# State sums for two quads at once, a last image kept on chip, and a new plan: a state-space layer and its feed-forward part on one core

## The chip, the core and the metric

One core of one Trainium2 chip. Times are device microseconds (us). TensorE is PE (PEld: its weight loads), VectorE DVE, ScalarE ACT, GpSimd POOL, SyncE SP; SP issues the DMA transfers. Every run named here was in the fast state. A ratio of two kernels is the mean time of one kernel's fast runs over that of the other's in the same rounds, so it is not quite the ratio of the medians that I quote.

## The reference, cut to what matters

```python
# x: (8, 384, 32, 32), all float32; per image 1024 tokens of 384 channels
t = layernorm(...)                                  # per token
xm, z = split(t @ in_proj_w.T)                      # 768 + 768
xc = silu(causal_conv3(xm))
dt, Bm, Cm = split(xc @ x_proj_w.T)                 # 24, 16, 16
dt = softplus(dt @ dt_proj_w.T + b)
h = exp(dt * A) * h + (dt * xc) * Bm                # scan over 1024 tokens, 768 x 16 states
y = (sum over the 16 states of h * Cm + xc * D) * silu(z)
x = x + gelu(y @ out_proj_w.T @ mlp_w1.T + b1) @ mlp_w2.T + b2
# images 0..4 only: binarised feed-forward with absmax quantisation, W1 (1536 x 384), W2 (384 x 1536)
```

## The kernel before

The kernel describes its work as operations with an engine, a cost and a priority. A greedy planner in the kernel simulates the engines, places every operation, and emits the instructions in that order. On the chip each engine then follows its own fixed order; semaphores make it wait for data and buffers. The planner's constants and its numbers of buffers therefore decide the order of everything.

```python
MM = 0.86; SWITCH = 0.34; BATCH = 1; IDLE = 0.7; SLACK = 1.0
# Plan.run, PE: a planned idle stretch above IDLE is filled with filler matmuls ("spare")
while now - free[e] > IDLE and ...: self.fill(); free[e] = clock.run(free[e], MM / 2)
# rings of buffers
"w_f": 4, "w_b": 4, "res": 3, "u": 6, "dt_r": 3, "dtx_r": 3, "front": 2, "yg": 1
"da": 2 (PSUM), "y": 1 (PSUM), "mm": 3 (PSUM)
```

The scan takes the 16 states in four quads. One tile has 32 channels x 4 states on its partitions:

```python
def scan_tile(...):
    ACT : da = exp(dt_r * a_neg)
    POOL: u = dtx_r * B
    DVE : to = tensor_tensor_scan(da, u)             # to is da, or u on a POOL tile
    DVE or POOL: u = to * C
# per quad: sum the 4 states of 32 channels; 4 column tiles of 32, fp32
def sums():
    for q, hcs in batch:                              # BATCH quads
        for p0, hc in parts:                          # 4 matmuls
            nc.tensor.matmul(py[p0:p0 + 32, :], self.fold, hc, start=(q == 0), stop=(q == 3))
add("PE", SWITCH + BATCH * MM, sums, ...)             # op.slack = SLACK
# then: xr = xr * D + py (DVE); xr = xr * z (POOL); store to yg_d in HBM
# s3: load yg from HBM; p_out: 3 x 6 matmuls; p_h: 36; p_o: 36 (per half image)
# s1: norms of both halves first; gates (p_z) late; x_proj and dt_proj weights resident in SBUF
[...]
```

Lines of lower priority fill PE between the sums: the projections of later images (p_in, p_z), out_proj and MLP of earlier ones (p_out, p_h, p_o), the feed-forward part (p_y). What is left of them when the last sums are done runs at the end.

## Time and profile before

| | before |
|---|---|
| median (3 runs) | 3439.42 us (3437.82 to 3448.25) |
| profiled span | 3444.9 us |
| busy PE / DVE / POOL / ACT | 96 / 84 / 77 / 59% |
| PE idle; fillers; half clock | 142 us; 128 us; PE busy 151 us at half rate |
| first sums, last sums | 130 us, 3345 us |

A group line names source line, engine, operation, tiles and shape, then the count, busy us, mean ns, and after the second bar the idle time of that engine before these instructions and who ended it. The prediction shows the lines. One more is needed later, from a table of windows; its columns are length, busy us of PE, PEld, DVE, ACT and POOL with counts, granted clock, DMA share, GB/s. It covers images 1 and 2 (from the first sums of image 1 to those of image 3) of the kernel before:

```profile
614.00:1424.00 810.00, 791.01 (x2610) 324.79 (x2606) 720.28 (x514) 477.22 (x488) 647.64 (x311) 0.99 0.68 224
```

PE is busy for 791 of 810 us here. It looks like the bound.

### The profile page before, as it was taken

Reading aid. Unit: us, or ns where it says so; the run is one execution under the profiler, and the core shown is the slowest. Engines: PE = TensorE matmul, PEld = TensorE weight load, DVE = VectorE, ACT = ScalarE, POOL = GpSimd, SP = SyncE. Lnnn points to the kernel's source line nnn. Section 1 sums busy time; section 2 is a strip of 40 time slices with the busy share of each in tenths; the row PEclk is TensorE's granted clock in tenths of the full one; section 3 lists DMA queues with packets and bytes.
Section 4 is the critical chain, followed back from the end, with each engine's and each line's share of the span. In section 5 each row is a group of like instructions: output and inputs, shape, how many; then the busy total and the mean of one; then the engine's idle time right before and its main releaser. Section 6 shows DMA issues by size and latency. Waiting matters only on the chain.

```text
span 3444.9 us, 32879 instructions
## 1 busy us (share of the span) xinstructions
PE 3302.8 (96%) x10500; PEld 1326.3 (38%) x10500; DVE 2885.8 (84%) x2193; ACT 2019.7 (59%) x2295; POOL 2655.3 (77%) x1288
## 2 busy tenths in 40 slices
PE   8888898999999999999999999999899999999999
PEld 3333433434343334333333333333333433333344
DVE  3577789899899989789989989899998899789870
ACT  4676567556666565554565656655576554555541
POOL 1778777777897968689777888788898779878850
PEclk9889899999999999999999999999999999999999
DMA  5876757667686557765588665986577666766542
GB/s 192 259 237 210 242 179 231 200 207 248 228 285 200 198 191 259 240 215 188 206 270 278 221 204 184 304 248 215 177 269 250 199 201 208 238 190 206 182 138 69
DMA packets 363965, 746.30 MB, mean 217 GB/s; under 512 B 34832, under 2 KB 103952, under 8 KB 363792
## 3 DMA queue, kind: packets, MB, share of 16 engines
q1 hardware_dynamic: 361776, 743.31, 66.6%
q8 instruction: 84, 1.38, 0.2%
q10 hardware_dynamic: 2016, 0.88, 0.1%
q14 instruction: 89, 0.73, 0.1%
HBM read 560.56 MB, written 183.50 MB: 216 GB/s over the span
## 4 chain that ended last, share of the span: by engine, by line
PE 61%; DVE 12%; DMA 8%; ACT 8%; POOL 5%; issue 5%; SPq 1%; DVEq 0%; POOLq 0%; ACTq 0%
PE p_y L454 14%; PE p_o L454 11%; PE p_h L454 10%; PE py L745 7%; DVE da L812 7%; PE p_out L454 6%; PE p_in L454 4%; PE p_z L454 4%; ACT da L470 3%; POOL u L808 2%; DVE u L825 2%; PE p_dbc L630 2%; ACT L470 1%; PE p_sum L483 1%; DMA dt_r<-dt_d 1%
## 5 line engine op out<-in xcount | busy, mean ns | idle before, releaser
L808 POOL TENSOR_TENSOR u<-dtx_r,bc 128x1024 f32<-128x1024 f32 x768 | 1796.8, 2359 | 493.7 <-PE py L745 418.9
L812 DVE TENSOR_TENSOR_SCAN da<-da,u 128x1024 f32<-128x1024 f32 (+1 forms) x576 | 1163.9, 2021 | 187.3 <-ACT da L470 113.0
L470 ACT ACTIVATE da<-dt_r,a_neg 128x1024 f32<-128x1024 f32 (+1 forms) x960 | 903.1, 946 | 687.8 <-DVE u L825 571.8
L825 DVE TENSOR_TENSOR u<-da,bc 128x1024 f32<-128x1024 f32 x576 | 703.2, 1221 | 25.2 <-DVE da L812 0.9
L454 PE MATMUL p_h<-t,w_b 128*128 128x512 f32 x1152 | 519.9, 601 | 12.2 <-ACT g L470 9.4
L454 PE MATMUL p_o<-g,w 128*128 128x512 f32 x1152 | 513.8, 598 | 1.2 <-DMA w<-in_mlp_w 1.0
L822 POOL TENSOR_TENSOR u<-u,bc 128x1024 f32<-128x1024 f32 x192 | 452.7, 2358 | 66.6 <-DVE u L812 46.1
L745 PE MATMUL py<-u,fold 128*32 128x512 f32 x3072 | 427.9, 611 | 15.7 <-POOL u L822 15.4
L812 DVE TENSOR_TENSOR_SCAN u<-da,u 128x1024 f32<-128x1024 f32 (+1 forms) x192 | 384.3, 2011 | 45.8 <-ACT da L470 29.8
L454 PE MATMUL p_y<-gf,w_n 128*128 128x512 f32 x720 | 328.9, 610 | 12.7 <-DMA w_n<-bin_w 8.2
L454 PEld LDWEIGHTS p_h<-t,w_b 128*128 128x128 f32 x1152 | 212.2, 190 | 315.0 <-issue 252.0
L454 PE MATMUL p_y<-tn,w_b 128*128 128x512 f32 x720 | 328.4, 605 | 1.0 <-ACT dt L470 0.8
L454 PEld LDWEIGHTS p_o<-g,w 128*128 128x128 f32 x1152 | 213.6, 190 | 299.9 <-issue 288.2
L470 ACT ACT_TABLE_LOAD x223 | 286.1, 1283 | 8.4 <-DVE xc L601 4.7
L454 PE MATMUL p_out<-yg,w 128*128 128x512 f32 x576 | 267.3, 616 | 16.8 <-DMA yg<-yg_d 9.6
L454 PE MATMUL p_in<-t,w_f 128*128 128x512 f32 x504 | 232.3, 608 | 10.3 <-ACT halo L596 6.0
L454 PE MATMUL p_z<-t,w_f 128*128 128x512 f32 x504 | 231.1, 607 | 2.3 <-ACT dt L470 1.3
L454 PEld LDWEIGHTS p_y<-gf,w_n 128*128 128x128 f32 x720 | 136.2, 194 | 204.0 <-issue 186.4
L454 PEld LDWEIGHTS p_y<-tn,w_b 128*128 128x128 f32 x720 | 134.1, 192 | 192.4 <-issue 154.0
L812 DVE TENSOR_TENSOR_SCAN da<-da,state,u 128x512 f32<-128x512 f32 x144 | 185.0, 1284 | 19.0 <-ACT da L470 7.0
L470 ACT ACTIVATE y<-p_y,v_b 128x512 f32<-128x512 f32 x150 | 101.8, 684 | 150.8 <-PE p_y L454 103.6
L601 DVE SCALAR_TENSOR_TENSOR xc<-p_in,conv_w,xc 128x511 f32<-128x511 f32 (+1 forms) x192 | 140.7, 742 | 54.2 <-ACT xc L470 32.6
(94 smaller groups left out, 2777.9 us busy)
## 6 DMA issues: line engine op xcount, KB each, us to landing
dtx_r<-dtx_d SPq DMA_DIRECT2D x144, 512.0 KB, 5.1
dt_r<-dt_d SPq DMA_DIRECT2D x144, 512.0 KB, 5.2
w_b<-in_mlp_w SPq DMA_DIRECT2D x192, 192.0 KB, 2.8
w<-in_mlp_w SPq DMA_DIRECT2D x96, 384.0 KB, 3.4
w_f<-in_in_proj_w SPq DMA_DIRECT2D x168, 192.0 KB, 4.5
y_d<-y SPq DMA_DIRECT2D x120, 256.0 KB, 3.8
gf<-y_d SPq DMA_DIRECT2D x20, 1536.0 KB, 9.2
xc_d<-xc SPq DMA_DIRECT2D x32, 768.0 KB, 7.5
```

What stands on the lines that cost most here:

```text
L454: self.nc.tensor.matmul(p.real, w.real[:, k, :], t.real[:, k0 + k, :], start=start and k == 0, stop=stop and k == n - 1,)
L470: lambda: self.nc.scalar.activation(out(), in_(), func, **{k: v() if callable(v) else v for k, v in kw.items()}),
L483: nc.tensor.matmul(p_sum.real, self.ones, t.real[:, k, :], start=(k == 0), stop=(k == KC - 1))
L601: nc.vector.scalar_tensor_tensor(xc.real[:, m, s:], pm.real[:, : T - s], tap[2 - s], xc.real[:, m, s:], ALU.mult, ALU.add,)
L630: nc.tensor.matmul(p_dbc.real, self.x_w[:, k, :], xc.real[:, k, :], start=(k == 0), stop=(k == KD - 1),)
L745: nc.tensor.matmul(py.real[p0 : p0 + DQ, :], self.fold, hc, start=(q == 0), stop=(q == NQUAD - 1),)
L808: add("POOL", 2.36, lambda: nc.gpsimd.tensor_mul(u.real, dtx_r.real, spread(bq)), r=[dtx_r, bq], w=[u])
L812: add("DVE", 0.13 + n * 0.0021, lambda k=k, col=col: nc.vector.tensor_tensor_scan(to.real[:, k, :], da.real[:, k, :], u.real[:, k, :], sta ...
L822: add("POOL", 2.36, lambda: nc.gpsimd.tensor_mul(u.real, u.real, spread(cq)), r=[cq], w=[u])
L825: add("DVE", 1.21, lambda: nc.vector.tensor_mul(u.real, da.real, spread(cq)), r=[da, cq], w=[u])
```

## The change

The intent: pay TensorE's change of tiling mode once for two quads; give the scan nine u tiles to make that possible, and find the memory for them by streaming the x_proj and dt_proj weights, by smaller rings and by dropping a constant tile (spread); spare the last image its trip of yg through HBM; warm TensorE's clock in the opening; move small work off DVE and POOL. The norm of a half and its gates move next to that half. All this is planned anew.

```diff
-BATCH = 1
+BATCH = 2
-SLACK = 1.0
+SLACK = 1.6
@@ Plan.run
+        free["PE"] = 2 * SIGNAL                       # fillers may stand in the opening
@@ rings
-"w_f": 4, "w_b": 4, "res": 3, "u": 6
+"w_f": 3, "w_b": 3, "res": 2, "u": 9
@@ s1
-        ts = [normed(half) for half in range(2)]      # gates: gate(0) in the second half, gate(1) last
+            t = normed(half)                          # per half, and gate(half, t) at its end
-            x_proj: resident self.x_w; dt_proj: resident self.dt_w
+            x_proj, dt_proj: two loads of 192 KB each through the r_w ring, per half
@@ last image
+                add("POOL", ..., tensor_mul(yg.real[:, m, :], xr.real, zr.real))   # yg stays on chip
+                self.matmuls(pm, w, yg, 0, KD - 1, True, False, ...)              # 5 of 6 k blocks early
+                self.matmuls(pm, w, yg, KD - 1, 1, False, True, ..., KD - 1)      # the last one late
@@ small
+ state copies of POOL tiles on POOL; centring as fused multiply-add on POOL; diagonal scaled on ACT
- self.spread (constants): broadcasts of ident and ones stand in for it, in the fillers too
[...]
```

More of the change, by code (lines that the diff above doesn't have):

```diff
@@ L335, in __init__ @@
         self.rings = {
-            "front": ring("front", 2), "t_f": ring("t_f", 2), "w_f": ring("w_f", 4),
+            "front": ring("front", 2), "t_f": ring("t_f", 2), "w_f": ring("w_f", 3),
             "dbc": ring("dbc", 1), "halo": ring("halo", 2),
-            "dt_r": ring("dt_r", 3), "dtx_r": ring("dtx_r", 3), "u": ring("u", 6),
+            "dt_r": ring("dt_r", 3), "dtx_r": ring("dtx_r", 3), "u": ring("u", 9),
             "xr": ring("xr", 1), "zr": ring("zr", 1), "state": ring("state", 1),
@@ L343, in __init__ @@
             "da": ring("da", 2, psum), "y": ring("y", 1, psum),
-            "yg": ring("yg", 1), "hid": ring("hid", 2), "t_b": ring("t_b", 1), "w_b": ring("w_b", 4),
-            "w6": ring("w6", 2), "w6_n": ring("w6_n", 2), "res": ring("res", 3),
+            "yg": ring("yg", 1), "hid": ring("hid", 2), "t_b": ring("t_b", 1), "w_b": ring("w_b", 3),
+            "w6": ring("w6", 2), "w6_n": ring("w6_n", 2), "res": ring("res", 2),
             "t_n": ring("t_n", 2), "small": ring("small", 12),
@@ L374, in __init__ @@
         self.plan.fill = lambda: self.nc.tensor.matmul(
-            self.plan.spare.real[:, : 2 * P], self.ones, self.spread[:, :2, :], start=True,
-            stop=True,
+            self.plan.spare.real[:, : 2 * P], self.ones,
+            self.ones.unsqueeze(1).to_broadcast([P, 2, P]), start=True, stop=True,
         )
@@ L394, in constants @@
         )
-        self.spread = const.tile([P, G, P], F32, name="spread")
-        for g in range(G):
-            nc.vector.tensor_copy(
-                self.spread[:, g, :], ident[:, g * DQ : g * DQ + 1].to_broadcast([P, P])
-            )
         self.edge = const.tile([P, KD, 2], F32, name="edge")
@@ L422, in constants @@
         nc.vector.tensor_scalar_mul(self.a_neg, self.a_neg, -1.0)
-        self.x_w = const.tile([P, KD, P], F32, name="x_w")
-        nc.scalar.dma_start(self.x_w, a["x_proj_w"])
-        self.dt_w = const.tile([P, DI], F32, name="dt_w")
-        nc.scalar.dma_start(self.dt_w, a["dt_proj_w"])
     def load(self, to, view, src, r=(), size=0, cost=0.4):
@@ L447, in weights, with matmuls @@
         return w
-    def matmuls(self, p, w, t, k0, n, start, stop, r, claim):
+    def matmuls(self, p, w, t, k0, n, start, stop, r, claim, w0=0):
         def emit():
@@ L454, in emit @@
                 self.nc.tensor.matmul(
-                    p.real, w.real[:, k, :], t.real[:, k0 + k, :],
+                    p.real, w.real[:, w0 + k, :], t.real[:, k0 + k, :],
                     start=start and k == 0, stop=stop and k == n - 1,
@@ L519, in spread @@
             for g in range(G):
+                one = self.ident[:, g * DQ : g * DQ + 1].to_broadcast([P, P])
                 nc.tensor.matmul(
-                    p_r.real[:, g * TG : (g + 1) * TG], self.spread[:, g, :], rstd.real,
-                    start=True, stop=True,
+                    p_r.real[:, g * TG : (g + 1) * TG], one, rstd.real, start=True, stop=True
                 )
@@ L565, in normed, with gate @@
             return t
-        def gate(half):
-            t = ts[half]
+        def gate(half, t):
             z = self.piece(r_z, [P, KD, T], "z")
@@ L579, in gate @@
             by_pair("z", half, z[0])
-        ts = [normed(half) for half in range(2)]
         for half, cols in enumerate(HALVES):
-            t = ts[half]
+            t = normed(half)
             xc = self.piece(r_x, [P, KD, T], "xc")
@@ L620, in s1 @@
             by_pair("xc", half, xc[0])
-            if half:
-                gate(0)
             p_dbc = self.piece("mm", [P, T], "p_dbc")
-            def x_proj(xc=xc, p_dbc=p_dbc):
-                for k in range(KD):
-                    nc.tensor.matmul(
-                        p_dbc.real, self.x_w[:, k, :], xc.real[:, k, :],
-                        start=(k == 0), stop=(k == KD - 1),
-                    )
             dbc = self.piece("dbc", [P, T], "dbc")
-            add("PE", KD * MM, x_proj, r=all_m, w=[p_dbc], claim=[dbc])
+            for i in range(2):
+                w = self.weights(r_w, KC, a["x_proj_w"][i])
+                self.matmuls(p_dbc, w, xc, i * KC, KC, i == 0, i == 1, all_m, [dbc])
             add("ACT", 0.59, lambda dbc=dbc, p_dbc=p_dbc: nc.scalar.copy(dbc.real, p_dbc.real),
@@ L643, in s1 @@
             for k in range(KD):
+                if k % KC == 0:
+                    w = self.weights(r_w, KC, a["dt_proj_w"][k // KC])
                 i = k % DTC * DQ
                 pd = self.piece("mm", [P, T], "p_dt")
-                add("PE", MM / 2, lambda i=i, k=k, pd=pd, dbc=dbc: nc.tensor.matmul(
-                    pd.real, self.dt_w[i : i + R, k * P : (k + 1) * P], dbc.real[i : i + R, :],
+                add("PE", MM / 2, lambda i=i, k=k, pd=pd, dbc=dbc, w=w: nc.tensor.matmul(
+                    pd.real, w.real[i : i + R, k % KC, :], dbc.real[i : i + R, :],
                     start=True, stop=True,
-                ), r=[dbc], w=[pd], claim=[dt])
+                ), r=[dbc, w], w=[pd], claim=[dt])
                 self.act(
@@ L662, in s1 @@
             self.store_all("dtx", b, half, xc, all_m)
-            if half:
-                gate(1)
+            gate(half, t)
     def store_all(self, name, b, half, t, parts):
@@ L678, in s2 @@
             state = self.piece("state", [P, NJ * NQUAD], "state")
+            if b == B - 1:
+                self.last_yg = [self.piece("front", [P, KD, T], "yg") for _ in range(2)]
             for half in range(2):
@@ L778, in scan @@
             ), r=[py], w=[xr])
+            if b == B - 1:
+                yg = self.last_yg[half]
+                add("POOL", c_pool(T), lambda m=m, xr=xr, zr=zr, yg=yg: nc.gpsimd.tensor_mul(
+                    yg.real[:, m, :], xr.real, zr.real
+                ), r=[xr, zr], w=[yg[m]])
+                continue
             add("POOL", c_pool(T), lambda xr=xr, zr=zr: nc.gpsimd.tensor_mul(
@@ L817, in scan_tile @@
             c0, step = cols[0], cols[1] - cols[0]
-            add("ACT", 0.25, lambda: nc.scalar.copy(
-                state.real[:, c0 : c0 + step + 1 : step], to.real[:, :, n - 1]
-            ), r=[to], w=[state[c0]])
+            kept, last = lambda: state.real[:, c0 : c0 + step + 1 : step], n - 1
+            if on_pool:
+                add("POOL", 0.12, lambda: nc.gpsimd.tensor_copy(kept(), to.real[:, :, last]),
+                    r=[to], w=[state[c0]])
+            else:
+                add("ACT", 0.25, lambda: nc.scalar.copy(kept(), to.real[:, :, last]),
+                    r=[to], w=[state[c0]])
         if on_pool:
@@ L833, in s3 @@
         for half, cols in enumerate(HALVES):
-            yg = self.piece("yg", [P, KD, T], "yg")
-            for i in range(2):
-                src = yg_d.real[i::2, half * DP : (half + 1) * DP, :]
-                self.plan.add("SP", 0.6, lambda i=i, yg=yg, src=src: nc.sync.dma_start(
-                    yg.real[i * DP : (i + 1) * DP, :, :], src.rearrange("k p l -> p k l")
-                ), r=[yg_d[half, m] for m in range(i, NP, 2)], w=[yg[i]], size=4 * DP * KD * T)
-            t2 = self.piece("t_b", [P, KC, T], "t2")
-            for m in range(KC):
-                w = self.weights("w6", KD, a["out_proj_w"][m])
-                pm = self.piece("mm", [P, T], "p_out")
-                self.matmuls(pm, w, yg, 0, KD, True, True, [yg[0], yg[1]], [t2])
+            t2 = self.piece("t_b", [P, KC, T], "t2")
+            if b == B - 1:
+                yg = self.last_yg[half]
+                late = []
+                for m in range(KC):
+                    w = self.weights("w6_n" if m == KC - 1 else "w6", KD, a["out_proj_w"][m],
+                                     r=[yg[KC]])
+                    pm = self.piece("mm", [P, T], "p_out")
+                    self.matmuls(pm, w, yg, 0, KD - 1, True, False,
+                                 [yg[k] for k in range(KD - 1)], [t2])
+                    late.append((w, pm))
+            else:
+                yg = self.piece("yg", [P, KD, T], "yg")
+                for i in range(2):
+                    src = yg_d.real[i::2, half * DP : (half + 1) * DP, :]
+                    self.plan.add("SP", 0.6, lambda i=i, yg=yg, src=src: nc.sync.dma_start(
+                        yg.real[i * DP : (i + 1) * DP, :, :], src.rearrange("k p l -> p k l")
+                    ), r=[yg_d[half, m] for m in range(i, NP, 2)], w=[yg[i]],
+                        size=4 * DP * KD * T)
+            for m in range(KC):
+                if b == B - 1:
+                    w, pm = late[m]
+                    self.matmuls(pm, w, yg, KD - 1, 1, False, True, [yg[KD - 1]], [t2], KD - 1)
+                else:
+                    w = self.weights("w6", KD, a["out_proj_w"][m])
+                    pm = self.piece("mm", [P, T], "p_out")
+                    self.matmuls(pm, w, yg, 0, KD, True, True, [yg[0], yg[1]], [t2])
                 add("ACT", 0.59, lambda m=m, t2=t2, pm=pm: nc.scalar.copy(
@@ L936, in means @@
             )
-            nc.vector.tensor_scalar_mul(mean.real, mean.real, 1.0 / (gs * kt * P))
+            nc.vector.tensor_scalar_mul(mean.real, mean.real, -1.0 / (gs * kt * P))
         add("DVE", c_dve(used) + 0.16, means, r=[sums], w=[mean])
@@ L948, in centre @@
                         wg = w.real[:, :, lo:hi]
-                        nc.gpsimd.tensor_scalar_sub(wg, wg, mean.real[:, g : g + 1])
-            add("POOL", 2.5, centre, r=[mean], w=[w])
+                        nc.gpsimd.tensor_scalar(
+                            wg, wg, 1.0, mean.real[:, g : g + 1], ALU.mult, ALU.add
+                        )
+            add("POOL", 1.8, centre, r=[mean], w=[w])
             sgn = self.piece("hid", [P, ks.stop - ks.start, ms.stop - ms.start], "sgn")
@@ L981, in quant_scale @@
         diag, p_max = self.piece("sq", [P, P], "diag"), self.piece("mm", [P, P], "p_max")
-        def spread_out():
-            nc.vector.tensor_reduce(m1.real, mx.real, AX.X, ALU.max)
-            nc.vector.tensor_scalar_mul(diag.real, self.ident, m1.real)
-        add("DVE", 0.4, spread_out, r=[mx[k] for k in range(n)], w=[m1, diag])
+        add("DVE", 0.17, lambda: nc.vector.tensor_reduce(m1.real, mx.real, AX.X, ALU.max),
+            r=[mx[k] for k in range(n)], w=[m1])
+        self.act(lambda: diag.real, lambda: self.ident, AF.Identity, c_act(P), r=[m1], w=[diag],
+                 scale=lambda: m1.real)
         add("PE", 0.25, lambda: nc.tensor.matmul(
@@ L1149, in _laid_out @@
     rows[DTC * DQ :] = xw[R:]
-    a["x_proj_w"] = rows.reshape(P, KD, P).transpose(2, 1, 0)
+    a["x_proj_w"] = rows.reshape(P, 2, KC, P).transpose(1, 3, 2, 0)
+    a["dt_proj_w"] = a["dt_proj_w"].reshape(P, 2, KC, P).swapaxes(0, 1)
     a["D_pair"] = np.tile(np.asarray(i[c + "D"]).reshape(NP, DP).T, (2, 1))
```

## The prediction

> **What bounds the kernel now.** I read the page's first two parts, then the groups of TensorE by form, the timeline of PE in a steady stretch and at the end, a table of windows by image, and last the waits. From the page of the kernel before:
>
> ```profile
> PE 3302.8 (96%) x10500; PEld 1326.3 (38%) x10500; DVE 2885.8 (84%) x2193; ACT 2019.7 (59%) x2295; POOL 2655.3 (77%) x1288
> ...
> PE   8888898999999999999999999999899999999999
> ...
> PEclk9889899999999999999999999999999999999999
> ```
>
> PE is busy for 96% of the span, and its low slices lie among the first seven, where the granted clock is low too. DVE, at 84%, is the nearest rival. The question is what fills PE's 3303 us. The groups of PE by form (busy us, mean ns, idle before them):
>
> ```profile
> L454 PE MATMUL p_o<-g,w 128*128 128x512 f32 x1152 | 513.8, 598 | 1.2 <-DMA w<-in_mlp_w 1.0 <-ACT g L470 0.2
> L745 PE MATMUL py<-u,fold 128*32 128x512 f32 x3072 | 427.9, 611 | 15.7 <-POOL u L822 15.4 <-DVE u L825 0.2
> ...
> L374 PE MATMUL spare<-spread,ones 128*128 128x256 f32 x522 | 128.4, 393 | 0.8 <-DVE t L526 0.7
> ```
>
> Each fp32 matmul is two records (1152 are 576 matmuls). The state sums (py) come as 384 groups of 8 records, four column tiles of 32 side by side. The fillers (spare) are 261 matmuls put where the planner saw an idle PE. Before the sums PE waits 15.7 us in all, so their data is nearly always there. The timeline of PE in a steady stretch (start us, length, instructions):
>
> ```profile
> 2002.05 1.06 PE L745 MATMUL py<-u,fold 128*32 128x512 f32 x8
> 2003.05 5.42 PE L454 MATMUL p_o<-g,w 128*128 128x512 f32 x12
> 2008.40 1.06 PE L745 MATMUL py<-u,fold 128*32 128x512 f32 x8
> 2009.39 5.42 PE L454 MATMUL p_o<-g,w 128*128 128x512 f32 x12
> ...
> 2015.74 10.57 PE L454 MATMUL p_o<-g,w 128*128 128x512 f32 x24
> 2026.23 1.07 PE L745 MATMUL py<-u,fold 128*32 128x512 f32 x8
> ```
>
> Twelve more records (24 against 12) cost 10.49 - 5.35 = 5.14 us: 0.4285 us each, 0.857 a matmul. But 12 records beside sums take 5.35, 0.21 more, and a group of sums takes 0.99 where two passes of 0.4285 are 0.857, so 0.13 more. **A switch to the sums and back costs 0.34 us.** Over the 380 groups at full clock the record starts give the same: 0.522 before a group, 0.996 for it, 0.533 for the next record; the excesses 0.094, 0.139 and 0.104 add up to 0.336.
>
> **Balance.** Counting PE's order with these units (3006 matmuls of 512 columns outside sums and filler at 0.857, 384 groups at 0.857 + 0.336, 78 variance groups at 0.55, 261 fillers at 0.43, the small rest) gives 3217 us of work at full rate. The span is 3445. The 228 us between are idle time (3445 - 3303 = 142) and half clock: the clock records have 176 us at half rate, PE busy in 151 of them, which loses 75. The sum is 217, so the balance closes to 11 us.
>
> **What the Trainium skill says.** (1) "TensorEngine Tiling (Array Packing)", Key Properties: changing the tiling mode, not merely the tile, drains TensorE. The trace agrees: weight loads are hidden inside a run, but at both ends of each group of sums 0.336 us is lost. (2) "TensorE: Matmul & The Clock Gate", Part 1: an idle window of about 3.4 us halves the clock until a busy one has passed. The trace agrees: record spacing is 0.429 or 0.853 us, and the half-rate stretches are multiples of 3.4 us, nearly half of their time before 614 us. (3) "Advanced Engine Details and Errata", VectorE Performance Modes: VectorE's two-port mode and GpSimd block each other on a shared port. The DVE scaling of a 128x128 diagonal runs from 0.286 to 2.49 us, median 1.31, in ten runs: consistent with blocking, though not proof.
>
> **The change, part by part.**
> 1. *Sums for two quads at once.* In the built order 384 groups of 4 matmuls become 192 groups of 8, and none of the old ones stood next to each other. The matmuls are the same. Saved: 192 x 0.336 = **64.5 us of PE time**, spread over the run, if the second quad's sums follow the first's in one mode without a stall.
> 2. *Fillers.* 261 become 189: 72 x 0.43 = **31 us** of PE time less. Of these 26 go at the end. Eleven stand in the opening, where PE waits for its first loads anyway; they cost nothing and lift the clock sooner. Before, the first two p_sum groups took 5.46 and 4.72 us for six records, against 2.74 later; I allow 4 us.
> 3. *Last image on chip.* The end before:
>
> ```profile
> 3344.49 1.06 PE L745 MATMUL py<-u,fold 128*32 128x512 f32 x8
> 3345.49 11.49 PE L374 MATMUL spare<-spread,ones 128*128 128x256 f32 x52
> 3360.15 18.73 PE L454 MATMUL p_out<-yg,w 128*128 128x512 f32 x36 [3.17 <-DMA yg<-yg_d]
> 3378.71 0.59 PE L374 MATMUL spare<-spread,ones 128*128 128x256 f32 x2
> 3379.14 31.06 PE L454 MATMUL p_h<-t,w_b 128*128 128x512 f32 x72
> ```
>
> From the last sums to p_h pass 34.65 us, of which 15.4 are p_out at full rate; the rest is the trip of yg to HBM and back, bridged by fillers, and a half-rate stretch. After, only the last of six k blocks waits for the last multiply (0.75 DVE and 1.27 POOL in this window), and 26 records of the first part's 30 and of the second part's six are left after the last sums: about 1.85 + 11.1 + 1 to 2 of waits = 14 to 15. So **about 20 us less at the end**: 11 are fillers counted in 2, 4 is p_out work moved ahead of the last sums, some 5 are idle time and half clock.
> 4. *Projection weights through the rings.* x_proj and dt_proj leave their resident tiles for 64 loads of 192 KB, 12.6 MB more than 746. DMA's share is about 0.7: hidden, near zero. What pays for nine u tiles is w_f and w_b from 4 to 3 buffers and res from 3 to 2. A w_b load lands in 2.8 us, w_f in 4.5, and two weights in hand last 2 x 2.57 = 5.1 us: enough unless the in-order queue blocks. I put **5 us of new waits** on it.
> 5. *Small moves.* Diagonal to ACT: 10 x 1.3 = 13 us of DVE. Centring as a fused multiply-add on POOL: 22 pieces of 1.04 to 2.6 us, probably halved, some 13 us of POOL in the first image. State copies of POOL's tiles go from ACT to POOL. All lie off PE.
>
> **Sum.** The same count over the changed order gives 3124 us of full-rate work, 94 less (64.5 + 31, to rounding). Losses: 228 - 5 (end) - 4 (clock in the opening) + 5 (rings) = 224. **3124 + 224 = 3348** profiled; the timed runs lie 5 us under it: 3343. I put 3345.
>
> **Rivals.**
> *DVE becomes the bound.* The table by image (PE, PEld, DVE, ACT, POOL busy):
>
> ```profile
> 614.00:1021.00 407.00, 398.24 (x1348) 169.97 (x1340) 359.41 (x264) 249.49 (x252) 336.39 (x166) 1.00 0.70 234
> ...
> 1810.00:2198.00 388.00, 382.75 (x1232) 149.82 (x1228) 352.85 (x250) 231.89 (x234) 322.60 (x154) 0.99 0.71 231
> ```
>
> From 614 to 2978 DVE works 2118 us of 2364 (90%). PE's order there falls from 2279 to 2209 us; with the 85 us of losses kept this makes 2294 and DVE, 13 us lighter, 92%. In single images it is tighter: the first after 614 has 352 us of PE order against DVE's 359, so that one cannot shrink in step. If DVE stops at 94%, the gain there halves: some 35 us lost, about 3380.
> *The second quad's wait takes the place of the switch.* The sums now need four u tiles, and a late one holds PE's in-order queue. Also, tiles are freed four at a time, and the waits show who depends on that:
>
> ```profile
> POOL u L808 <- PE py L745: 418.9, 158, 12.3
> ```
>
> For it: POOL already stands 419 us waiting for tiles. Against: nine tiles less the four in a batch leave five, before six less two left four; and the plan's slack before sums rises from 1.0 to 1.6 us. Sums waited 15.7 us before; doubling that gives 3360.
> *Fewer fillers mean a colder clock.* If half rate grew by 60 us, 30 would be lost: 3375. Against: the fillers went because the new plan has less idle time to fill.
> *Better than the sum.* The first image (130 to 614 us) loses 54 us idle and 82 us at half clock, and its order changes: gates now follow each half, POOL is lighter. If half of that 95 us loss goes: 3300.
>
> **Range and chances.** The switch saving is measured 380 times and I trust it within 10%; the fillers and the end are counted. What is uncertain is the 224 us of losses: +-20% is 45 us. That gives 3297 to 3390. The 2% line is 3371, 26 us above my figure: the DVE rival alone crosses it, so faster 0.77, within 2% 0.22, slower 0.01 (all gains would have to be more than repaid).
>
> **What would show it.** Groups of sums: 192 of 16 records, about 1.85 us apiece from first start to next start (1.71 + 0.14), and py's busy time near 427.9 - 192 x 0.14 to 0.25 = 380 to 400. Spare records 378, some 80 to 95 us. End from last sums to p_h 14 to 15 us, no yg load. PE idle near 140, half clock below 176 us, DVE near 86% of the span. It would be wrong if PE's idle before py rises far above 16 us, if DVE passes 93% from 614 us to the last sums, or if PE waits for w_f or w_b loads by tens of us.

## The result, and the profile after

| | before | after |
|---|---|---|
| median | 3443.03 us (4 runs) | 3401.94 us (4 runs, 3395.41 to 3411.99) |
| ratio | | 0.9883, interval 0.9853 to 0.9914 |
| profiled span | 3444.9 us | 3393.6 us |
| granted clock | 0.975 | 0.971 |

The change gains 1.2%. The prediction had 3345 us and a range of 3297 to 3390; the result lies above it. The page of the changed kernel:

```profile
PE 3213.9 (95%) x10356; PEld 1331.2 (39%) x10356; DVE 2875.2 (85%) x2179; ACT 2017.5 (59%) x2278; POOL 2644.4 (78%) x1312
...
PE   8987898999898999799999999999999999999999
```

PE is busy 89 us less, yet the span is only 51 us shorter. The groups of PE by form:

```profile
L729 PE MATMUL py<-u,fold 128*32 128x512 f32 x3072 | 381.3, 611 | 5.4 <-POOL u L816 5.4
...
L375 PE MATMUL spare<-ones 128*128 128x256 f32 x378 | 100.7, 408 | 1.3 <-DVE eps_f L400 1.1
```

The sums are 46.6 us cheaper in busy time (the prediction had 28 to 48), and PE waits less before them than it did. In the timeline of PE the batch is what was wanted:

```profile
1864.49 1.92 PE L729 MATMUL py<-u,fold 128*32 128x512 f32 x16
1866.34 5.42 PE L444 MATMUL p_y<-tn,w_b 128*128 128x512 f32 x12
```

Sixteen records take 1.85 us to the next start. Over the batches at full clock the median is 1.854: four passes of 0.4285 and 0.14 of switch, no stall between the quads. The end:

```profile
3314.17 1.92 PE L729 MATMUL py<-u,fold 128*32 128x512 f32 x16
3316.02 4.56 PE L444 MATMUL p_out<-yg,w 128*128 128x512 f32 x10
...
3327.29 0.59 PE L375 MATMUL spare<-ones 128*128 128x256 f32 x2
3327.72 31.06 PE L444 MATMUL p_h<-t,w_b 128*128 128x512 f32 x72
```

From the last sums to p_h are 13.55 us (34.65 before), and from the last record of the sums to the end of the kernel 78 instead of 100 us (the tables below count the end so).

So both large parts are there. What is missing shows in the same windows of images 1 and 2 as above, from the changed kernel:

```profile
628.00:1436.00 808.00, 751.20 (x2474) 311.24 (x2476) 721.85 (x516) 477.03 (x495) 649.29 (x312) 0.95 0.69 228
```

PE is busy 40 us less and is idle for it. The stretch takes 808 us where it took 810, with DVE's 722 us of work and POOL's 649 as before. PE's 98% had not meant that PE set the pace here.

A ledger of PE makes this exact. Idle time is the span less PE's busy time; fillers are the busy time of spare; half clock is half of PE's busy time (fillers apart) inside the half-rate clock records, the time lost there; work is the rest, that is real work at full rate with its switches.

| kernel | span | work | idle | fillers | half clock |
|---|---|---|---|---|---|
| before | 3444.9 | 3101.9 | 142.1 | 128.4 | 72.5 |
| after | 3393.6 | 3038.4 | 179.7 | 100.7 | 74.8 |
| difference | -51.3 | -63.5 | +37.6 | -27.7 | +2.3 |

The work fell by the 64 us of the switches. The other three columns are loss; together they went from 343 to 355 us. The end alone brought them down by some 18 us (22 at the end before, 4.5 after), so **outside the end the loss grew by about 30 us**. The prediction had them fall.

The growth has a place. By stretch between first sums, the loss went from 22 to 33 us in the opening, from 128 to 121 in image 0, from 72 to 110 in images 1 and 2, and from 100 to 87 in images 3 to 7. These last five images took 1880 us where they took 1921. So the saving was lost in images 1 and 2 and in the opening, not everywhere. And PE's idle time changed its kind; the waits of PE in the changed kernel begin with

```profile
PE p_y L444 <- ACT gf L460: 21.8, 3, 13.1
PE p_in L444 <- DMA w_f<-in_in_proj_w: 12.1, 8, 3.0
...
PE p_h L444 <- DMA w_b<-in_mlp_w: 9.4, 3, 5.9
```

(us in all, times, longest). PE waited 1.2 us for gf, the input of the feed-forward part, before, and 21.8 now, 19.1 of it in images 1 and 2. Its waits for weight loads of all rings went from 15.2 to 43.5 us. Its waits for the loads of x in the opening (18.4 us before) are gone, and those before the sums fell.

### The profile page after: what moved, and what is told of

It reads as the page before. It is cut to its first block, busy times and chain, and to the rows that moved or that the text cites. A ratio compares the mean times of both kernels' runs of the same rounds, so it can differ in the third digit from the quotient of the medians.

```text
span 3393.6 us, 32501 instructions
## 1 busy us (share of the span) xinstructions
PE 3213.9 (95%) x10356; PEld 1331.2 (39%) x10356; DVE 2875.2 (85%) x2179; ACT 2017.5 (59%) x2278; POOL 2644.4 (78%) x1312
## 4 chain that ended last, share of the span: by engine, by line
PE 63%; DVE 10%; DMA 9%; ACT 9%; POOL 4%; issue 3%; SPq 1%; ACTq 0%; DVEq 0%; POOLq 0%
PE p_y L444 16%; PE p_o L444 11%; PE p_h L444 10%; PE py L729 7%; DVE da L802 6%; PE p_out L444 6%; PE p_z L444 5%; PE p_in L444 4%; ACT da L460 3%; POOL u L798 2%; ACT L460 2%; DVE u L819 2%; DMA w_f<-in_in_proj_w 1%; PE spare L375 1%; PE p_dt L628 1%
## 5 line engine op out<-in xcount | busy, mean ns | idle before, releaser
L819 DVE TENSOR_TENSOR u<-da,bc 128x1024 f32<-128x1024 f32 x576 | 703.1, 1221 | 18.4 <-ACT state L813 0.9
L729 PE MATMUL py<-u,fold 128*32 128x512 f32 x3072 | 381.3, 611 | 5.4 <-POOL u L816 5.4
L444 PE MATMUL p_y<-gf,w_n 128*128 128x512 f32 x720 | 324.8, 606 | 26.4 <-ACT gf L460 21.8
L444 PE MATMUL p_out<-yg,w 128*128 128x512 f32 x552 | 250.9, 607 | 9.9 <-ACT da L460 4.2
L590 DVE SCALAR_TENSOR_TENSOR xc<-p_in,conv_w,xc 128x511 f32<-128x511 f32 x192 | 141.1, 742 | 58.7 <-ACT halo L585 37.6
L729 PEld LDWEIGHTS py<-u,fold 128*32 128x32 f32 x3072 | 81.7, 110 | 273.4 <-issue 199.4
```

The source lines that it names most:

```text
L444: self.nc.tensor.matmul(p.real, w.real[:, w0 + k, :], t.real[:, k0 + k, :], start=start and k == 0, stop=stop and k == n - 1,)
L590: nc.vector.scalar_tensor_tensor(xc.real[:, m, s:], pm.real[:, : T - s], tap[2 - s], xc.real[:, m, s:], ALU.mult, ALU.add,)
L729: nc.tensor.matmul(py.real[p0 : p0 + DQ, :], self.fold, hc, start=(q == 0), stop=(q == NQUAD - 1),)
L819: add("DVE", 1.21, lambda: nc.vector.tensor_mul(u.real, da.real, spread(cq)), r=[da, cq], w=[u])
```

## The experiments

Two theories after the first look. *Bound by PE*: PE's work sets the time, and new waits (smaller rings, streamed weights) ate 47 us. *Bound by the order*: in each engine's fixed order the sums advance at a pace that no single engine's load sets; PE's loss is what this pace leaves, and the planner's order decides how much. Kernels named a_ are the changed kernel with an edit, b_ the kernel before with one. "Same order" means that the planner's costs were left alone, so the instructions stand where they stood. Times of a_ kernels are set against the changed kernel's median, 3401.94 us; the kernel before, timed in every group of rounds, had medians from 3442.2 to 3447.8, so differences across groups are good to about 5 us.

### Putting the switch back, same order: a_switch

```diff
+                    for n_q, (q, hcs) in enumerate(batch):
+                        if n_q:
+                            nc.tensor.matmul(py.real[:, :4], self.zeros, self.ones[:, :4], start=False, stop=False)
```

> The changed kernel, same order on every engine, with one matmul of 4 columns by a full 128x128 block of zeros put between the two quads of each batch: the tiling mode switches again in the middle (result unchanged). PE gets 192 x 0.336 us of switches back, plus 192 x 0.05 to 0.1 us for the small matmul: 75 to 85 us. If PE sets the time, as the prediction took it, the kernel takes about 3402 + 70 to 85 = 3472 to 3487 us. If idle time of PE swallows part (PE waits on other engines between), it gains clearly less: 20 to 50 us, 3422 to 3452.

3460.42 us, 58 more than the changed kernel. The timeline of PE:

```profile
2009.75 1.06 PE L736 MATMUL py<-u,fold 128*32 128x512 f32 x8
2010.75 0.39 PE L724 MATMUL py<-ones,zeros 128*128 128x4 f32 x2
2011.06 1.06 PE L736 MATMUL py<-u,fold 128*32 128x512 f32 x8
2012.06 1.13 PE L630 MATMUL p_dt<-dbc,w_f 24*128 24x512 f32 x6
```

A batch with the forced switch takes 2.31 us where it took 1.85. The ledger's work rises by 79.7 us, of which idle time swallows 27.5, while half clock adds 10: span +62.5. Both expectations missed: it lies between them. Added PE work, put into the sums, is paid at about three quarters of its size.

### Taking PE work away, same order: a_pe_cut, b_pe_cut

The p_o matmuls but the first of each group work on 352 of 512 columns.

```diff
+                c = 352 if p.name == "p_o" and not (start and k == 0) else T
-                    p.real, w.real[:, w0 + k, :], t.real[:, k0 + k, :],
+                    p.real[:, :c], w.real[:, w0 + k, :], t.real[:, k0 + k, :c],
```

> The changed kernel, same order, 11 of the 12 matmuls of each p_o (528 in all) cut from 512 to 352 columns: a wrong result on purpose, 528 x 2 x 160 columns x 0.837 ns = 141 us of PE work less. PE sets the time: 3402 - 120 to 141 = about 3261 to 3282 us. The scan chain (ACT, POOL, DVE) and other waits set it at least half of the time: PE idle grows by 70 us or more and the time falls by less than 70, to 3335 or more.

3391.53 us: 10 us gained. (The comparison with the reference still passed; its tolerance does not see this cut.) The page of a_pe_cut:

```profile
PE 3128.7 (92%) x10356; PEld 1346.9 (40%) x10356; DVE 2875.2 (85%) x2179; ACT 2017.4 (60%) x2278; POOL 2645.0 (78%) x1312
```

The ledger's work fell by 124 us, idle time grew by 80, half clock by 40. The last sums stand at 3319 us, as in the changed kernel (3315.5); all that was gained lies behind them, where the p_o of the end is shorter.

> The kernel before, same order, p_o matmuls cut as in a_pe_cut (141 us of PE work less, a wrong result on purpose). If PE set the time of the kernel before, as the prediction read from its 96%: 3442 - 100 or more. If the sums' pace set it there as well: less than 30 us gained, most of it in the end, where only PE works (48 of 72 matmul halves of p_o there are cut by 31%: 8 us).

3424.11 us against 3447.76 of its rounds: 24 us by the medians, 18 by the ratio (0.9948, interval 0.9929 to 0.9967), of a cut that the ledger puts at 118. The last sums come 14.5 us earlier, the end is 10 shorter. So the kernel before was not bound by PE's whole load in its fixed order either. That it was is the reading that the prediction began with.

Work added costs three quarters, work removed returns a tenth to a fifth. The two tests do not touch the same work: the switch stands in the sums, on which POOL waits for tiles, and p_o stands between them. Whether that makes the difference was not tested.

### Taking DVE and POOL work away, same order: a_dve_cut, a_pool_cut, a_both_cut, a_three_cut

```diff
-            add("DVE", 1.21, lambda: nc.vector.tensor_mul(u.real, da.real, spread(cq)),
+            add("DVE", 1.21, lambda: nc.vector.tensor_mul(u.real[:, :, :c], da.real[:, :, :c], spread(cq)[:, :, :c]),
# c: three quarters of the columns; the cut of POOL's last multiply is of the same kind
```

> The changed kernel, same order, the last DVE multiply of each scan tile (576 of 1.22 us) done on three quarters of the columns: a wrong result on purpose, about 576 x 0.267 = 154 us of DVE work less. PE sets the time: under 20 us gained, 3382 or more. The chain through DVE sets it: 60 us or more gained, 3342 or less. If both share it, 20 to 60 us.

3388.26 us, 14 gained of 144 that DVE's busy time fell: it is not DVE either.

> The changed kernel, same order, with both cuts at once: 141 us less PE work in p_o and 154 us less DVE work in the last multiply (wrong result on purpose). Alone they gave 10 and 14 us. If PE and DVE bound it together, each standing right behind the other, both gain far more than 24 us: 60 or more, 3342 or less. If the order's waits on ACT, POOL and DMA hold it, about 24 to 35 us: 3367 or more.

3358.29 us, 44 gained. That is more than 10 + 14, so PE and DVE do stand behind each other, but it missed both ranges: less than the 60 that joint binding would have made, more than 35. The page of a_both_cut:

```profile
PE 3114.7 (93%) x10356; PEld 1344.7 (40%) x10356; DVE 2727.4 (81%) x2179; ACT 2016.1 (60%) x2278; POOL 2641.7 (79%) x1312
```

> The changed kernel, same order, POOL's last multiply of its own scan tiles (192 of 2.36 us) on three quarters of the columns: a wrong result on purpose, about 192 x 0.57 = 110 us of POOL work less. If POOL sets the pace: 50 us or more gained, 3352 or less. If it stands in line with the others, as PE and DVE do: 5 to 20 us, 3382 to 3397.

3403.00 us: nothing from POOL alone.

> The changed kernel, same order, all three cuts: 141 us of PE, 154 of DVE, 110 of POOL less (wrong result on purpose). PE and DVE together gave 44 us. If the three stand behind each other: clearly more, 70 to 110 us, 3292 to 3332. If other waits (ACT, DMA, buffers) hold the order: 44 to 60 us, 3342 to 3358.

3357.48 us: with 131 us of PE work and 146 and 106 us of DVE and POOL busy time less, the gain stays at 44. What holds the order then is something that these cuts left alone: other waits (ACT, DMA landings, the two PSUM tiles of da) or other work of the same three engines. I did not separate them. In a fixed order most of one engine's saving turns into its own idle time.

### No fillers, same order: b_nofill

```diff
-                    self.fill()
```

> The kernel before, same order, without its 261 filler matmuls (128 us of PE busy time). If fillers cost what they are busy, as the prediction counted for the 72 that the change drops, the time falls by some 112 us. If they only stand in time in which PE would have waited anyway, it stays within 15 us, or grows by the half clock that they kept off (up to 60 us).

3445.56 us against 3442.22, ratio 1.0007 (0.9997 to 1.0018). The page of b_nofill:

```profile
PE 3203.4 (93%) x9978; PEld 1236.5 (36%) x9978; DVE 2885.8 (84%) x2193; ACT 2020.4 (59%) x2295; POOL 2656.7 (77%) x1288
```

All 128 us of fillers are gone, but none of the time: idle time takes 93 us of them and half clock 23. In this order fillers are idle time in another form. The prediction's term for those outside the end, 46 of them at 0.43 us, was never there to be saved.

### The end alone: b_tail

The diff is the "last image" part of the change, on the kernel before.

> The kernel before with one part alone: the last image's gated outputs stay on chip and out_proj runs in two parts. The prediction's 20 us at the end should stand by themselves: 3442 - 20 = 3422 us, with the stretch from the last sums to the first p_h near 14 us and the rest of the span as before. If the new plan gives them back elsewhere: within 10 us of 3442.

3425.15 us against 3445.29, ratio 0.9937: 20 us by the medians, as the prediction had it. The timeline of PE at its end:

```profile
3342.81 1.06 PE L747 MATMUL py<-u,fold 128*32 128x512 f32 x8
3343.80 8.85 PE L454 MATMUL p_out<-yg,w 128*128 128x512 f32 x20
...
3359.79 31.06 PE L454 MATMUL p_h<-t,w_b 128*128 128x512 f32 x72
```

The last sums stand about where they stood (3343 us, 3345 before), and it is the end that is shorter, 82 us for 100.

### The batch alone, and all but the batch: b_batch2, a_batch1

```diff
-BATCH = 1
+BATCH = 2        # b_batch2, six u tiles;  a_batch1 is the reverse on the changed kernel
```

> The kernel before with sums for two quads at once and nothing else (six u tiles, slack 1.0). If the switches saved are PE time that sets the end: 3442 - 50 to 64 = 3378 to 3392. If six u tiles, four of them held for a batch, choke POOL and DVE: POOL's waits for py rise above 419 us and the time is 3442 or more.

3866.04 us, 12% slower. The waits of b_batch2:

```profile
POOL u L808 <- PE py L745: 692.7, 162, 10.9
ACT da L470 <- DVE u L825: 674.6, 255, 13.5
DVE da L812 <- POOL u L808: 372.4, 141, 17.4
```

A batch holds four of six u tiles; POOL, then DVE, then ACT stand waiting in turn (419, 65 and 572 us for the same three before). So more tiles are not an extra but a condition of the batch (seven and eight were not tried), and the memory for them must come from somewhere.

> The changed kernel with sums for one quad at a time (the rest kept, planned anew). Putting the switches back in the same order cost 58 us, so 3402 + 58 = 3460 if the two-quad batch carries the gain; if the planner works round the switches, as it did in the kernel before, 3410 to 3430 (the end's 20 us below before), and the batch is worth little in a plan that knows of it.

3477.35 us, 75 more than the changed kernel, and even 32 more than the kernel before, which lacks the shorter end. Its last sums come at 3271 us, 44 earlier than in the changed kernel, but then PE works off what was left behind; the windows of a_batch1:

```profile
3271.00:3470.00 199.00, 195.04 (x462) 86.18 (x454) 7.51 (x10) 36.26 (x39) 1.27 (x1) 1.00 0.28 88
```

PE works alone for 199 us where the changed kernel needs 78. The ledger has 3091 us of work (+53) and 379 us of loss (+24). Both expectations missed, on the slow side. So the remaining parts, planned with single quads, are worse than the kernel before; whether by a cost of their own or by the order is asked next.

### More buffers behind the same order: a_wf4

The plan counts three w_f buffers, the memory has four; a smaller descriptor area pays for the fourth.

```diff
-dynamic_dma_scratch_size=1024
+dynamic_dma_scratch_size=256
+REAL = {"w_f": 4}          # buffers of the real ring; the plan keeps 3
```

> The changed kernel, same order on every engine, but four buffers behind the w_f ring in place of three (the plan still counts three): loads of in_proj, x_proj and dt_proj weights may start one buffer sooner. PE stood 19 us waiting for them. If these waits took the gain: PE's idle before p_in, p_z, p_dt on w_f loads falls to under 5 us and the time falls by 15 us, to 3387. If the order sets it: within 5 us of 3402.

3400.21 us, 2 less than the changed kernel. PE's waits for w_f loads before p_in, p_z and p_dt came down from 19 to about 16 us only. The physical lack of a w_f buffer does not explain 30 us. But since the waits hardly fell (for all weight loads together they stayed, 43.5 and 44.5 us), this run does not tell what they cost. The reverse, the old order with the small rings, deadlocked in the check and was not run. A third res buffer does not fit into memory; a fourth w_b buffer in place of the fourth w_f passes the check, but was not run.

### The same kernels in other orders: b_slack105, b_slack16, a_slack12

```diff
-SLACK = 1.0
+SLACK = 1.05     # b_slack105;  1.6 in b_slack16;  a_slack12: 1.6 -> 1.2
```

Slack is no instruction. It shifts when the planner thinks that sums are ready, and so the order.

> The kernel before with the planner's slack before sums at 1.05 us in place of 1.0: no instruction is added or dropped but fillers, only the order changes. Theory: the order found by the greedy planner is itself worth some 30 us either way, and the kernel before has a lucky one: 3442 + 20 to 40. Rival: the order is a small matter, and something that the change adds (smaller rings, streamed projection weights, later norms) costs the 50 us: within 8 us of 3442.

3474.70 us against 3443.01: **0.05 us of slack cost 32 us.**

> The kernel before with the change's slack of 1.6 us alone. If the longer slack itself costs (sums planned later, tiles held longer), the time grows steadily with slack: more than at 1.05, 3442 + 40 to 60. If only the draw of the order matters, it lies anywhere from 3442 to 3490 and not in order of the slack.

3487.46 us. This time the order of the slacks is kept.

> The changed kernel with slack 1.2 in place of 1.6. If slack costs by itself, 1.2 is faster than 1.6: 3402 - 10 or so. If the order's draw decides and 1.6 was chosen as a lucky one, it is slower by 20 to 70 us: 3422 to 3472.

3454.00 us, 52 more than at 1.6. In the changed kernel a longer slack is not what costs. The ledgers (end: from the last record of the sums):

| kernel | span | work | idle + fillers + half clock | last sums | end |
|---|---|---|---|---|---|
| before (1.0) | 3444.9 | 3101.9 | 343 | 3345 | 100 |
| b_slack105 | 3472.5 | 3104.6 | 368 | 3363 | 110 |
| b_slack16 | 3491.6 | 3094.2 | 397 | 3393 | 99 |
| after (1.6) | 3393.6 | 3038.4 | 355 | 3316 | 78 |
| a_slack12 | 3448.0 | 3045.5 | 403 | 3312 | 137 |

Work stays within 11 us in each family; **the order moves the loss by 25 to 54 us.** The kernel before has the best draw of its three, the changed kernel the better of its two. In a_slack12 the sums are done 4 us earlier than in the changed kernel and the whole difference lies at the end.

### Undoing the move of norms and gates, in three orders: a_gate16, a_gate12, a_gate085

```diff
-            t = normed(half)
+        ts = [normed(half) for half in range(2)]      # and gate(0), gate(1) in the second half, as before
```

> The changed kernel (slack 1.6) with norms of both halves first and the gates after, as before the change. If moving them costs the missing 30 us: 3402 - 30 = 3372. If the order's draw decides, undoing a part of a plan that was tuned as a whole makes it slower by 30 to 70 us: 3432 to 3472.

> The same at slack 1.2, to compare with the changed kernel at slack 1.2 (3454). If moving the norms and gates costs 30 us: 3424, the same difference as at slack 1.6. If the draw decides: the difference has another size or sign than at slack 1.6; about 3410.

At slack 1.6 undoing it makes the kernel 62 us slower (3463.69 against 3401.94); at slack 1.2 it makes it 36 us faster (3417.99 against 3454.00). One part of the change has no size of its own that such a swap could show.

> The same at slack 0.852, chosen among some hundred slacks because the kernel's own plan ends earliest. If choosing the order is worth as much as the parts: the fastest of all, 3380 to 3392, with the same full-rate PE work of about 3038 us as the changed kernel and less idle time, filler and half clock (340 us against 360). If the plan's own end says little about the chip: anywhere from 3400 to 3450.

3392.64 us, ratio to the kernel before 0.9849 (0.9832 to 0.9865), the fastest median of all kernels that compute the right thing. It lies 0.6 us above the slow edge of what was expected. Its work is 3038.5 us, the same as the changed kernel's 3038.4; its loss is 352 us against 355 (idle 157, fillers 127, half clock 68). It was picked only because the kernel's own plan ended earliest among some hundred slacks, and it beats the changed kernel by 9 us; the two intervals overlap slightly, so I count it as equal or a little better.

Three things in these traces bear on what the order does. First, in all five orders of the changed kernel with two-quad sums (1.6, a_slack12 and the three of this section) the last sums come within 12 us (3312 to 3323), while the end takes 74 to 137 us: 78, 137, 137, 103 and 74. There the draw decides mostly how much other work is left over when the sums are done. Second, one wait does not follow the draw: PE waits 43 to 47 us for weight loads in these five, 15, 23 and 22 in the three orders of the kernel before. It belongs to the change (streamed weights, smaller rings); how much of it costs time, and how much fills idle time that PE would have had anyway, is not shown. Third, where the norms of both halves come first, the time rises with the slack each time (1.0, 1.05, 1.6; and 0.852, 1.2, 1.6); only with the norms per half is 1.6 faster than 1.2. That slack costs by itself in the former is not excluded.

## Why the prediction was wrong, point by point

- *Switches: right.* 192 of them, 0.336 us each: 64.5 predicted, work fell by 63.5, the batch took 1.854 us, and the sums waited less, not more (5.4 us for 15.7). The rival of the second quad's wait did not come.
- *The end: right.* 20 us predicted; 22 in the changed kernel, 20 alone in b_tail.
- *Fillers: wrong.* "72 x 0.43 = 31 us of PE time less" was booked as a saving. b_nofill shows that in the kernel before the fillers are worth nothing in time. The 11 us of those at the end were real, but only as part of the end's 20; the 20 us of the 46 elsewhere were not.
- *The step that failed: "Losses: 228 - 5 (end) - 4 (clock in the opening) + 5 (rings) = 224".* I took idle time and half clock as a fixed tax on PE, carried over and corrected by single waits. They measured 254.5 us in the changed kernel (214.6 before; 228 was what the count of the order left over). The first half of the sum held: work and fillers together fell by 91 us of the 93 counted. The losses rose by 40 where a fall of 4 was counted, and these 44 of the 46 us between forecast and profile are the miss. They are not fixed: the orders of the same work moved them by tens of us, and taking 118 to 124 us of work from PE raised idle time and half clock by 94 to 121. Images 1 and 2 took 808 us for 810 with 40 us less PE work: the saving became idle time there.
- *The two corrections inside that step.* "+ 5 (rings)": PE's waits for weight loads rose by 28 us, those on w_f and w_b from 2.3 to 28.6. This is the sign of being wrong that the prediction named ("by tens of us"), and it came; "enough unless the in-order queue blocks" did not hold. How much of it reached the time is open: a_wf4 returned 2 us, but hardly lowered the waits. "- 4 (clock in the opening)": the half-clock loss before the first sums went from 5.3 to 4.9 us only, and the first sums came at 144 us for 130; with two quads they also come at 143 in b_batch2, and with one at 124 in a_batch1.
- *Behind it, the reading of the bound.* 96% busy was read as "PE sets the time". b_pe_cut: 118 us of work less, 24 us gained. The page "Perfetto Trace Analysis", section Identifying the Most-Contended Engine, warns that matmul occupancy is no good measure of TensorE's headroom. b_pe_cut agrees with the warning. The share that the page points to instead, that of weight loads, would not have helped: it is 38% here, and where p_o runs without a gap the timeline shows one load of 0.19 us per 0.43 us, 44%. The page's advice to optimise the most occupied engine first did not carry in these fixed orders: neither PE nor DVE nor POOL alone gave more than 24 us.
- *The rival "DVE becomes the bound"* saw that the first image after 614 us "cannot shrink in step", and it shrank by 12 us only (the next one grew by 9). But it made DVE's load the reason, and a_dve_cut gives 14 us. Its 3380 was nearer than the sum and still too low.
- *A slip in the reading.* Of the half-rate stretches before, 96 of 176 us lie before 614 us: more than half of their time, not "nearly half". The sum does not rest on it.
- *What stays open.* Of the 30 us by which the loss grew outside the end, I cannot say how many belong to streamed weights, smaller rings or moved norms, and how many to the draw of the order. The waits for weight loads (28 us more, in every order) and for gf (21 us more, in this one) are the leads. But orders of the same work differ by as much or more, and the one part that I swapped in two orders changed sign.

## What to carry to other kernels

Before booking a saving on the busiest engine, ask what its idle time and fillers are: if they are the slack against a pace that another engine or the order sets, the saving lands there. Test it cheaply by cutting work from that engine without touching the order. When a plan is made anew, compare what PE waits for before and after, too: a wait that is there in every order belongs to the change. And where a greedy planner makes the order, change one of its harmless constants first: the spread of these times (here 30 to 50 us, 1 to 1.5%) is the size below which no single comparison tells what a part of a change is worth.

## What the Trainium skill lacked or had wrong

- "TensorEngine Tiling (Array Packing)", Key Properties, says that changing the tiling mode drains TensorE, without a price. Here: 0.336 us for going from 128x128 to 128x32 and back (0.094 before, 0.139 in the group, 0.104 after it), and 0.45 us more per batch, the small matmul included, when a matmul of 4 columns forces it in between (medians 2.307 against 1.854 us).
- "Perfetto Trace Analysis", Identifying the Most-Contended Engine, has the engine of highest occupancy optimised first, TensorE being judged by its weight loads. With orders fixed on five engines this did not hold: cuts of 124 us on PE (matmuls 95%, weight loads 39%), 144 us on DVE (85%) and 105 us on POOL (78%) gave 10, 14 and 0 us, all three together 44.
- "TensorE: Matmul & The Clock Gate" (Why this matters for your kernels) says to keep idle gaps of TensorE short. No page that I read says what fillers are worth in a kernel that interleaves other engines: here 261 of them (128 us busy) kept 23 us of half-clock loss away, and the time was the same without them (ratio 1.0007).
- No page has this (it would belong to "GPSIMD Engine Reference"): on POOL the centring of 304 columns took 1044 ns as a plain subtraction of a per-partition scalar and 524 ns as a fused multiply and add (medians).
